# Products of the identity in TensorE's planned waits, and the rows of two more batches turned by VectorE and memory

## The chip, the cores and the metric

The kernel runs on one core of a Trainium2 chip. The metric is the time of one execution on the device, in microseconds (us); the median of several runs is quoted. The "granted clock" is the share of full speed that the profile shows for TensorE. "PSUM" is the program's name for the memory, in banks, that its TensorE products write to. Where two kernels are compared, "ratio" is the mean time of one kernel's runs over the mean of the other's runs of the same rounds on the same chip, so it is not quite the ratio of the medians; the 95% interval stands in brackets. "Start" and "last product" are times from the start of the profiled span.

## The reference

It is a stack of four graph-network layers on 32 batches of 512 nodes with 128 features, in float32. Every layer normalizes the rows, applies relu, calls a graph layer and adds the result to its input:

```python
for layer in (L0, L1, L2, L3):
    h = jnp.maximum(_layernorm(x), 0.0)
    x = x + layer(h, adj)
# L0: leaky_relu(norm(adj + I) @ (h @ W) + b)
# L1: elu(h @ W_in), elu(h @ W_out), elu(h @ W_node); adj @ in, adj.T @ out; tanh(concat @ W_upd)
# L2: four layers of row- and column-normalized adj with src, dst and self parts, with skips
# L3: m = tanh(adj @ (h @ W_msg)), then a GRU step of (m, h)
```

## The kernel before

The batches are independent. The program records every operation with its engine, an estimated duration and the buffers it uses; a list scheduler (`order`) then plans one order for all engines, in which the operations of several batches are mixed, and emits them in that order. In the trace of this kernel TensorE's 9594 records stand exactly in the planned order, also where the chip is slower than the plan (a wait of 1.29 us for `agg_in`, where the plan has no gap over 0.7 us) or faster (no wait ahead of the second and third fold, where it has one).

```python
class Plan:
    def op(self, engine, us, emit, reads=(), writes=(), kb=0.0, rank=None, later=0.0, land=0.0): ...
    def order(self):                       # an event loop: the engine that is idle takes the ready
        ...                                # operation of the lowest key that finds free buffers
        return done
```

Layers 1 to 3 need the normalized rows `h` also transposed, as `hT`. There are two ways to it. At the ends, where few batches are in flight, four TensorE transposes and a copy by ScalarE do it; in this kernel's trace the record of one transpose is 273 ns in the median, three in a row start 0.11 us apart, and the copy takes 0.59 us. In the middle VectorE turns 32x32 blocks (0.71 us for 128x512), four writes to memory (1.8 us each in the median, from issue to landing) and one read (2.7 us) put the blocks in their places, and ScalarE copies (0.62 us):

```python
        at_ends = b < 3 or b >= B - 2

        def transposed(h, name):
            if at_ends:
                ps, hT = plan.bank("t"), buf("s2", name=name)
                for c in range(NC):
                    op("PE", 0.109, lambda c=c: nc.tensor.transpose(ps.ap()[:, c * P:(c + 1) * P], h.ap()[:, c, :], ident),
                       [(h, {c}), ID], [(ps, {c})])
                op("ACT", t_act(N), lambda: nc.scalar.copy(hT.ap(), ps.ap()), [ps], [hT])
                return hT
            t, hT = turned(h, "turned"), buf("s2", name=name)
            op("ACT", t_act(N), lambda: nc.scalar.copy(hT.ap().rearrange("p (c a r) -> p c a r", c=NC, a=NC), turned_cols(t)), [t], [hT])
            return hT
```

One piece of layer 1 comes up later: ScalarE brings the sums `agg_in` and `agg_out` out of PSUM, for the products `upd`, and also copies the `rows` of norms, which only layer 2 needs.

```python
        op("ACT", t_act(N), lambda: nc.scalar.copy(agg_in.ap(), psi.ap()), [psi], [agg_in])
        ...
        op("ACT", t_act(2 * N), lambda: nc.scalar.copy(
            rows.ap().rearrange("p s (c n) -> p (s c) n", c=NC), spaced.ap().rearrange("p n k -> p k n")), [spaced], [rows])
```

## Time and profile before

| what | before |
|---|---|
| time, median of 3 runs | 2331.95 us (2329.25 to 2332.02) |
| profiled span | 2328.9 us |
| TensorE busy | 2293.4 us |
| TensorE's first real product | 11.06 us |
| end of TensorE's last product | 2321.50 us |
| mean granted clock | 0.997 |

TensorE is busy 98% of the span, so its own time line can be kept like an account. From the first real product to the end of the last one there are 2321.50 - 11.06 = 2310.4 us. Of these 2293.4 are busy, and the remaining 17.0 are waits. The tail after the last product is 7.4 us. The lines of the profile are in the prediction below, with how they are read; a line of the time line gives the start, the length, the engine and the line of the program, the operation, and in square brackets the idle time ahead of it and who ended it.

### The profile page before, as it was taken

The page shows a single profiled execution, that of the slowest core. Times are in us where ns is not written, and L with a number is a line of the kernel's source. Part 1 is how long each engine was busy: PE and PEld are TensorE (multiplying, and loading weights), DVE is VectorE, ACT ScalarE, POOL GpSimd, SP SyncE. Part 2 cuts the span into 40 slices and gives each one's busy share as a digit, 9 for nine tenths or more (in the row PEclk, how much of TensorE's full clock was granted, in tenths as well). Part 3 has the DMA queues.
Part 4 walks back from the last instruction along what each step waited for, and adds up shares of the span by engine and source line. Part 5 has one row for each costly group of instructions (what it writes and reads, how often), then busy time and mean ns, then how long its engine had stood idle before and what let it go on. Part 6 is the DMA issues. An engine that isn't in the chain of part 4 may idle for free.

```text
span 2328.9 us, 28035 instructions
## 1 busy us (share of the span) xinstructions
PE 2293.4 (98%) x9594; PEld 1438.1 (62%) x9594; DVE 1519.9 (65%) x4124; ACT 935.0 (40%) x2018; POOL 284.2 (12%) x218
## 2 busy tenths in 40 slices
PE   6999999999999999999999999999999999999998
PEld 4666666566665666666666666666656666666565
DVE  5556567666676776757766676666667667576754
ACT  7323434344343444434444333443434444344512
POOL 3001101111110111101111011111011111011101
PEclk9999999999999999999999999999999999999999
DMA  6202222323323133222233223232231332323100
GB/s 215 81 1 86 68 74 81 109 64 100 98 83 109 46 109 104 90 87 82 78 104 100 74 90 109 64 100 91 80 116 50 109 96 91 94 64 113 50 5 10
DMA packets 127295, 196.63 MB, mean 84 GB/s; under 512 B 18352, under 2 KB 75184, under 8 KB 127152
## 3 DMA queue, kind: packets, MB, share of 16 engines
q1 hardware_dynamic: 126864, 194.71, 27.2%
q8 instruction: 76, 1.25, 0.2%
q14 instruction: 67, 0.55, 0.1%
q10 hardware_dynamic: 288, 0.13, 0.0%
HBM read 157.95 MB, written 36.83 MB: 84 GB/s over the span
## 4 chain that ended last, share of the span: by engine, by line
PE 91%; DVE 3%; issue 2%; DMA 2%; ACT 1%; POOL 1%; SPq 0%; DVEq 0%; POOLq 0%; ACTq 0%
PE ps_agg L295 60%; PE ps_seven L566 12%; PE ps_sd L295 9%; PE ps_upd L295 3%; PE ps_gate L295 2%; PE ps_msg L295 1%; PE ps_lin L295 1%; PE ps_node L295 1%; DMA x<-in_x 0%; POOL inv L690 0%; ACT h L447 0%; DVE bn L419 0%; SPq L465 0%; DMA turned<-turn_turned 0%; DVE z L637 0%
## 5 line engine op out<-in xcount | busy, mean ns | idle before, releaser
L295 PE MATMUL ps_agg<-aT,sd 128*128 128x512 f32 x1024 | 509.6, 593 | 1.8 <-DVE sd L544 1.0
L295 PE MATMUL ps_agg<-a,sd 128*128 128x512 f32 x1024 | 489.4, 593 | 0.0
L435 POOL TENSOR_TENSOR sc<-v,neg_half 128x4 f32<-128x4 f32 (+1 forms) x128 | 170.0, 1328 | 1630.8 <-DVE v L422 1053.3
L295 PEld LDWEIGHTS ps_agg<-a,sd 128*128 128x128 f32 x1024 | 181.7, 190 | 158.3 <-issue 148.8
L447 ACT ACTIVATE h<-xr,nb,sc 128x128 f32<-128x128 f32 x384 | 158.2, 482 | 294.0 <-DVE nb L443 290.2
L295 PE MATMUL ps_agg<-f,w_sb 128*128 128x512 f32 x448 | 229.4, 594 | 0.0
L295 PEld LDWEIGHTS ps_agg<-aT,sd 128*128 128x128 f32 x1024 | 177.5, 191 | 75.1 <-issue 62.0
L295 PE MATMUL ps_sd<-w_sb,f 128*128 128x256 f32 x768 | 221.6, 381 | 1.8 <-ACT f L485 1.3
L566 PEld LDWEIGHTS ps_seven<-t_sb,s 128*128 128x128 f32 x1128 | 164.2, 191 | 67.9 <-issue 56.2
L295 PEld LDWEIGHTS ps_sd<-w_sb,f 128*128 128x128 f32 x768 | 137.5, 192 | 107.4 <-issue 85.0
L522 DVE TENSOR_TENSOR sd<-ps_sd,rf_sb 128x512 f32<-128x512 f32 x128 | 88.2, 689 | 145.2 <-PE ps_sd L295 144.5
L566 PE MATMUL ps_seven<-t_sb,s 128*128 128x128 f32 x1128 | 177.2, 275 | 0.0
L737 ACT ACTIVATE f<-ps_agg,cf_sb 128x512 f32<-128x512 f32 x128 | 87.4, 683 | 145.3 <-PE ps_agg L295 145.0
L295 PE MATMUL ps_agg<-aT,rep 128*128 128x512 f32 x256 | 130.9, 593 | 2.6 <-DVE rep L662 1.4
L295 PE MATMUL ps_agg<-a,rep 128*128 128x512 f32 x256 | 130.7, 592 | 0.0
L295 PE MATMUL ps_agg<-aT,msg 128*128 128x512 f32 x256 | 127.6, 593 | 0.0
L566 PEld LDWEIGHTS ps_seven<-w_sb,f 128*128 128x128 f32 x512 | 83.5, 191 | 55.7 <-issue 47.1
L690 POOL TENSOR_TENSOR inv<-stat,neg_half 128x8 f32<-128x8 f32 x32 | 64.7, 2022 | 370.5 <-DVE stat L689 370.5
L592 DVE TENSOR_TENSOR ev<-ps_seven,ev 128x512 f32<-128x512 f32 x94 | 64.6, 688 | 65.0 <-PE ps_seven L566 63.5
L607 ACT ACTIVATE sq<-a 128x512 f32<-128x512 f32 x128 | 79.9, 624 | 51.7 <-DMA a<-in_adj 50.3
L295 PE MATMUL ps_agg<-aT,h 128*128 128x256 f32 (+2 forms) x384 | 99.7, 380 | 0.0
L295 PEld LDWEIGHTS ps_agg<-f,w_sb 128*128 128x128 f32 x448 | 78.4, 191 | 27.8 <-issue 20.3
(142 smaller groups left out, 3781.9 us busy)
## 6 DMA issues: line engine op xcount, KB each, us to landing
aT<-in_adjt SPq DMA_DIRECT2D x124, 512.0 KB, 5.7
a<-in_adj SPq DMA_DIRECT2D x62, 512.0 KB, 5.5
turn_turned<-blk SPq DMA_DIRECT2D x324, 64.0 KB, 1.8
turned<-turn_turned SPq DMA_DIRECT2D x81, 256.0 KB, 2.7
spaced<-bounce SPq DMA_DIRECT2D x32, 512.0 KB, 4.8
x<-in_x SPq DMA_DIRECT2D x32, 256.0 KB, 2.8
out<-xo SPq DMA_DIRECT2D x30, 256.0 KB, 2.1
turn_f4r<-blk SPq DMA_DIRECT2D x108, 64.0 KB, 1.8
```

The costliest lines, as they stand in the source:

```text
L295: op("PE", t_mm(n), lambda: nc.tensor.matmul(out_of(ps.ap()), lhs(), rhs(), start=start, stop=stop), reads, [ps], later=later)
L435: op("POOL", t_pow(n), lambda: nc.gpsimd.tensor_tensor(inv.ap()[:, :n], v8.ap()[:, :n], neg_half[:, :n], op=ALU.pow), [v8, NH], [(inv, {0})])
L447: op("ACT", t_act(D, 2), lambda c=c: nc.scalar.activation(h.ap()[:, c, :], xin.ap()[:, c, :], AF.Relu, bias=nb.ap()[:, c:c + 1], scale=inv ...
L522: op("DVE", t_tt(N), lambda ps=ps, h=h: nc.vector.tensor_add(sd.ap()[:, 2 * h:2 * h + 2, :], ps.ap().rearrange("p (j v) -> p j v", j=2), s ...
L566: op("PE", t_mm(D), lambda j=j: nc.tensor.matmul(ps.ap()[:, k * H + j * D:k * H + (j + 1) * D], lhs()[:, j * P:(j + 1) * P], rhs(), start= ...
L592: op("DVE", t_tt(N), lambda: nc.vector.tensor_add(ev.ap(), bank_b.ap()[:, None, :H].to_broadcast([P, 2, H]), ev.ap()), [bank_b, ev], [ev])
L607: op("ACT", 0.73, lambda c=c: nc.scalar.activation(sq.ap(), a.ap()[:, c, :], AF.Copy, accum_out=stat.ap()[:, c:c + 1]), [(a, {c})], [sq, ( ...
L690: op("POOL", t_pow(2 * NC), lambda: nc.gpsimd.tensor_tensor(inv.ap(), stat.ap(), neg_half, op=ALU.pow), [stat, NH], [inv])
L737: op("ACT", t_act(N, 1), lambda ps=ps, i=i, f_new=f_new: nc.scalar.activation(f_new.ap(), ps.ap(), AF.Tanh, bias=cf_sb[:, i:i + 1]), [ps, ...
```

## The change

It has two parts. First, wherever the plan leaves TensorE idle for over 0.7 us, products of the identity with itself are emitted, as many as the plan says fit, into a PSUM bank that is free then; the result is never read. Their intent is to keep TensorE's clock up. `WARM` and `COLD` in the diff are the pace of one product: in before's trace the two records of a fold product take 0.22 us, from start to start, at full pace and 0.43 at half. `RISE` is the estimate of how long half pace lasts, where that trace has 5.5, 3.5 and about 6.8 us; `SHORT` is a choice. Second, batches 2 and 30 take the way through VectorE and memory, with 16 TensorE transposes fewer in each.

```diff
+    WARM, COLD, RISE, SHORT = 0.2225, 0.428, 3.5, 0.7
+    def kept_warm(self, done, product, begin):
+        banks = {x for o in done for x in o.bufs if x.kind == "bank"}
+        out, at, cold = [], begin, self.RISE
+        for o in done:
+            if o.engine == "PE":
+                gap = o.ready - at
+                if gap > self.SHORT:
+                    n = int(min(gap, cold) / self.COLD + max(gap - cold - 0.1, 0.0) / self.WARM)
+                    cold = 0.0
+                    used = {x.slot for x in banks if x.since < o.ready and x.until > at - 0.1}
+                    slot = next((k for k in range(self.places["bank"]) if k not in used), None)
+                    if slot is not None:
+                        out.append((slot, n))
+                at = o.ready + o.us
+            out.append(o)
 ... (emits out; the event loop notes o.ready, x.since and x.until)
-        at_ends = b < 3 or b >= B - 2
+        at_ends = b < 2 or b >= B - 1
 ...
+    def idle_products(slot, n):
+        ps = psum.tile([P, N], F32, name="ps_idle", tag=f"bank_{slot}", bufs=1)
+        for _ in range(n):
+            nc.tensor.matmul(ps[:, :P], ident, ident, start=True, stop=True)
 ...
-        for o in plan.order():
-            o.emit()
+        plan.kept_warm(plan.order(), idle_products, 1.3)
```

More of the change, by code (lines that the diff above doesn't have):

```diff
@@ L193, in order @@
                             free[buf.kind].append(buf.slot)
+                            buf.until = now
                     unfinished[o.batch] -= 1
@@ L209, in order @@
                     for x in new:
-                        x.slot = free[x.kind].pop(0)
+                        x.slot, x.since, x.until = free[x.kind].pop(0), now, None
                 for item in held:
@@ L215, in order @@
                 done.append(o)
+                o.ready = now
                 idle_at[e] = now + o.us
@@ L225, in order @@
         return done
+    WARM, COLD, RISE, SHORT = 0.2225, 0.428, 3.5, 0.7
[14 more added lines that the diff above has]
+            out.append(o)
+        for o in out:
+            if isinstance(o, tuple):
+                product(*o)
+            else:
+                o.emit()
 @with_exitstack
```

## The prediction

> **What bounds the kernel now.** I read four views in this order: busy times, TensorE's waits, the windows with the granted clock, and TensorE's timeline at the two ends. The first is the page's line of busy time.
>
> ```profile
> PE 2293.4 (98%) x9594; PEld 1438.1 (62%) x9594; DVE 1519.9 (65%) x4124; ACT 935.0 (40%) x2018; POOL 284.2 (12%) x218
> ```
>
> TensorE (PE) is busy 98% of a span of 2328.9 us, so its 35.5 us without work are nearly all that waiting can give back. The view of waits, cut to TensorE and the first 60 us, shows where most of them lie:
>
> ```profile
> PE ps_fold L295 <- DMA raw<-in_raw: 11.1, 1, 11.1
> PE ps_t L483 <- ACT h L447: 4.5, 2, 3.1
> PE ps_lin L295 <- ACT agg L632: 1.4, 2, 0.7
> PE ps_upd L295 <- ACT agg_in L667: 1.3, 1, 1.3
> PE ps_agg L295 <- DVE v L609: 1.1, 1, 1.1
> PE ps_sd L295 <- ACT hT L485: 0.8, 1, 0.8
> PE ps_sd L295 <- ACT f L485: 0.7, 1, 0.7
> ```
>
> 11.1 us are the first load, some 9.8 are waits in batches 0 to 2. From 60 to 2170 us the same view lists only 2.8 us; from 2170 on it has 4.1 us (1.4 on `rep`, the rest under 0.8 each), and after TensorE's last product, at 2321.5, comes a tail of 7.4 us that the change does not touch. In the middle nothing is to be had but TensorE's own work.
>
> Busy is not full speed. Windows (stretch, length, busy time and count of PE, PEld, DVE, ACT, POOL, then the clock):
>
> ```profile
> 30.00:33.50 3.50, 3.50 (x8) 2.75 (x9) 0.97 (x3) 2.55 (x8) 0.00 (x0) 0.52 0.87 250
> 55.40:61.00 5.60, 4.90 (x10) 2.90 (x11) 4.29 (x27) 5.34 (x14) 2.61 (x3) 0.52 0.64 154
> 61.00:90.00 29.00, 29.00 (x88) 15.56 (x87) 15.95 (x39) 15.60 (x31) 3.30 (x2) 1.00 0.39 141
> ```
>
> In two stretches the granted clock is 0.52. A third is not in that column (1.00 there), but the timeline shows it. Each float32 product has two records, so x12 is six products:
>
> ```profile
> 11.06 2.93 PE L295 MATMUL ps_fold<-raw 128*128 128x128 f32 x12 [11.06 <-DMA raw<-in_raw]
> ...
> 21.72 1.50 PE L295 MATMUL ps_fold<-raw 128*128 128x128 f32 x12
> ...
> 30.00 3.68 PE L295 MATMUL ps_sd<-w_sb,hT 128*128 128x256 f32 x8 [0.75 <-ACT hT L485]
> ...
> 76.16 1.03 PE L295 MATMUL ps_sd<-w_sb,hT 128*128 128x256 f32 x4
> ```
>
> Six products of one form take 2.93 us at 11 us and 1.50 at 22, that is about 0.43 and 0.22 us each from start to start. The half pace lasts from 11.06 to about 16.6.
>
> [...] half pace for 5.5, 3.5 and about 6.8 us. [...] it was at half clock at 30.0 us after gaps of 1.41 and 0.75 us, not one long gap. [...] VectorE's turn (0.711 us for 128x512) needs four writes to memory of 1.8 us and a read of 2.7 us after it, from issue to landing. [...] records here are 273 ns, but three in a row start 0.11 us apart, and that is the cost to the stream.
>
> **The change, part by part.** The built program's order shows 79 products of the identity: 33 ahead of the first real product, then groups of 3, 4, 5, 4, 5, 6 and 10 in batches 0 to 2, and 5 and 4 near the end. 32 transposes leave TensorE (80 before, 48 after), 8 turns are added on VectorE (108 to 116). Nothing else is added to TensorE.
>
> (1) Clock. First stretch: 5.5 us at half pace become 2.75, provided inputs are there: the last part of `h` is done at 14.26 and of `diag` at 14.24, and the chunk that needs them would start at about 16, so yes. Gain 2.75. Second: the four `sd` products take 3.50 us from start to start; warm, at 0.43 each, 1.72. Gain 1.8. Third: from 57.73 to 61.07, 3.34 us hold products that need 1.72 warm; the transposes before them run at ScalarE's pace and gain nothing. Gain 1.6. Sum 6.15 us. The chain of batch 0 runs from TensorE through ScalarE and VectorE back to TensorE here, so I count all of it.
>
> (2) What the products of the identity cost where they are too many. The identity is ready at 1.34 us. If the clock rises after 3.5 us, 33 products take 8 x 0.428 + 25 x 0.2225 = 9.0 us and end at 10.6, before the load at 11.02; if after 6.8 us, 16 x 0.428 + 17 x 0.2225 = 10.6, ending at 12.2. I take a loss of 0.35. The groups of 4 and 5 ahead of the second and third fold are 2.0 us, where the trace shows no wait at the folds and 1.41 just after: loss 0.6. 4 ahead of `sd` are 0.9 against a wait of 0.75, 6 ahead of `lin` 1.3 against 0.68, before a long gap anyway: together 0.35. Loss 1.3; (1) and (2) leave 4.85.
>
> (3) Transposes: 32 x 0.11 = 3.5 us off an engine that is never idle in between. The turns add 8 x 0.711 = 5.7 us to VectorE (65% busy), and their wait of some 6 us lies behind other batches' products, as for batches 3 to 29 now.
>
> (4) Waits. I built the products of the identity alone, without the turns, to read its order: 90 products, among them 14 where now are 10, a group of 4 after that which is gone, and 5, 4 and 3 near the end where now are 5 and 4. The first real product after the 10 is now batch 2's own aggregation, moved up because its path has become longer. So 11 products, 11 x 0.2225 = 2.4 us, is what the new order expects to wait less. The trace's waits at those places (3.07 and 0.67 near 55 us, 3.9 from 2180 to 2200) make it plausible. I take 2.2.
>
> Sum: 4.85 + 3.5 + 2.2 = 10.6 us, 0.45%. 2331.95 - 10.6 = 2321.4; I say 2321.
>
> **The rivals.**
> (a) A wait takes the place of the one removed: in the first 60 us the end is set by loads and by ScalarE, not TensorE. For: ScalarE is busy 9.68 of 10 us from 40 to 50 and 9.18 from 50 to 60, memory moves over 400 GB/s from 11 to 20. Against: ScalarE waits 0.95, 0.44 and 1.76 us between 30 and 40 for results that come earlier now, and the loads of batch 1 are in by 24. It would cut (1) to half: 2324 to 2325.
> (b) The products of the identity get in the way: they stand in program order, and a real product that is ready earlier has to wait. For: the groups ahead of the folds. Against: 46 of them after the start are 10.2 us in all and replace waits of 9.8 + 4.1. All in the way by a third: 2324.
> (c) The turns of batches 2 and 30 add waits of 5 to 6 us where too few batches are in flight. For: batch 30 has only batch 31 beside it at the end. Against: batch 31 is at work then, and the order has just one planned gap there. If two turns show: 2331.
> (d) The clock stays low in spite of them, so that (1) is lost and only 4 us remain: 2328. Against: they are ordinary products.
>
> **Range and chances.** The three times before span 2.8 us. Each rival takes 3 to 10 us and none is likely to hold in full; the other way, waits at both ends could shrink by 4 more. So 2315 to 2327. Two per cent is 46.6 us, more than all of TensorE's idle time: same is nearly certain.
>
> **What would show it.** Right: no clock under 0.9 between 11 and 90 us; the four first `sd` products in 1.9 us; the first fold at 11 to 12 us; batch 0's aggregation done near 17.5 instead of 20; 48 transposes; TensorE's waits of the first 60 us mostly filled; the waits from 2170 on cut from 4.1 us to about 2. Wrong: the first fold later than 12.2; `ps_sd` or `ps_msg` waiting for `turned` in batch 2 or 30 for over 2 us; a mean clock under 0.99 from 20 to 60 us; TensorE's last product less than 6 us earlier than 2321.5.

## The result

The changed kernel took 2319.45 us (2317.86 to 2320.76, 6 runs) against 2330.71 us of the kernel before in the same rounds. The ratio is 0.9951 [0.9938, 0.9964]: 0.5% faster, within the 2% that count as the same. In the profile the span went from 2328.9 to 2316.1 us, the mean clock from 0.997 to 0.999. The page's line of busy times, after:

```profile
PE 2301.4 (99%) x9720; PEld 1450.3 (63%) x9720; DVE 1521.2 (66%) x4132; ACT 933.6 (40%) x2018; POOL 284.1 (12%) x218
```

TensorE is busy 8.0 us longer although the span is 12.8 us shorter, because the products of the identity count as busy. The view of waits of the first 60 us had seven lines before, the first of them the 11.1 us of load. What is left of it now, whole:

```profile
PE ps_idle L862 <- POOL ident masks.py:199: 1.4, 1, 1.4
PE ps_upd L324 <- ACT agg_in L696: 1.2, 1, 1.2
PE ps_agg L324 <- ACT h L476: 0.8, 1, 0.8
```

TensorE's time line, at the three stretches that ran at half clock before, shows the 33 first products (66 records), the folds, and the `sd` products:

```profile
1.40 9.96 PE L862 MATMUL ps_idle<-ident 128*128 128x128 f32 x66 [1.40 <-POOL ident masks.py:199]
11.41 1.61 PE L324 MATMUL ps_fold<-raw 128*128 128x128 f32 x12
...
28.22 1.99 PE L324 MATMUL ps_sd<-w_sb,hT 128*128 128x256 f32 x8
```

Six fold products take 1.61 us instead of 2.93, and the `sd` products 1.99 instead of 3.68. The windows (clock third from the end) agree, with 1.00 where there was 0.52:

```profile
30.00:33.50 3.50, 3.44 (x17) 2.17 (x16) 3.50 (x16) 3.42 (x9) 1.19 (x1) 1.00 0.97 323
55.40:61.00 5.60, 5.60 (x24) 3.65 (x23) 3.18 (x11) 5.35 (x16) 0.19 (x2) 1.00 0.74 254
```

Near the end, where batch 30 starts, TensorE's time line before was:

```profile
2180.53 1.16 PE L295 MATMUL ps_lin<-w_sb,agg 128*128 128x128 f32 x8 [0.68 <-ACT agg L632]
2182.34 1.48 PE L483 MATMUL ps_t<-ident,h 128*128 128x128 f32 x4 [0.65 <-ACT h L447]
2184.50 1.13 PE L295 MATMUL ps_sd<-w_sb,f 128*128 128x256 f32 x4 [0.68 <-ACT f L485]
...
2197.30 1.10 PE L295 MATMUL ps_agg<-aT,rep 128*128 128x512 f32 x2 [1.45 <-DVE rep L662]
...
2299.54 1.40 PE L483 MATMUL ps_t<-ident,h 128*128 128x128 f32 x4
```

and after:

```profile
2179.17 1.28 PE L862 MATMUL ps_idle<-ident 128*128 128x128 f32 x10
2180.29 1.03 PE L324 MATMUL ps_sd<-w_sb,f 128*128 128x256 f32 x4
...
2187.23 1.05 PE L324 MATMUL ps_lin<-w_sb,agg 128*128 128x128 f32 x8
...
2294.38 0.60 PE L512 MATMUL ps_t<-ident,h 128*128 128x128 f32 x4
```

The four waits in brackets are gone, and so are both groups of transposes that took 1.48 and 1.40 us. Four transposes without a wait take 0.60 us, as the last line shows. Before, they took so long because ScalarE delivered `h` in four pieces: at 2182.34 the four records of 0.328 us start 0.38 us apart, beside ScalarE's 1.65 us for the pieces. This is waiting that the profile counts as busy.

**The account of TensorE.** "Products" are those of the identity after the first group, at 0.2225 us each; "work" is the busy time without any of them; "waits" is the rest up to the last product. The account is made from one profile of each kernel and adds up to the last product.

| kernel | first real product | work | waits | products | last product |
|---|---|---|---|---|---|
| before | 11.06 | 2293.4 | 17.0 | 0 | 2321.5 |
| after | 11.41 | 2281.2 | 5.8 | 10.2 | 2308.7 |

So the gain of 12.8 us in the profile is nearly all in the work (-12.2). Waits and products together are 16.0 us where the waits alone were 17.0.

### The profile page after: what moved, and what is told of

It is laid out like the page before. It is cut to its first block, busy times and chain, and to the rows that moved or that the text cites.

```text
span 2316.1 us, 28365 instructions
## 1 busy us (share of the span) xinstructions
PE 2301.4 (99%) x9720; PEld 1450.3 (63%) x9720; DVE 1521.2 (66%) x4132; ACT 933.6 (40%) x2018; POOL 284.1 (12%) x218
## 4 chain that ended last, share of the span: by engine, by line
PE 92%; DVE 3%; DMA 2%; ACT 1%; SPq 1%; issue 1%; POOL 0%; DVEq 0%; ACTq 0%; POOLq 0%
PE ps_agg L324 60%; PE ps_seven L595 12%; PE ps_sd L324 9%; PE ps_upd L324 3%; PE ps_gate L324 2%; PE ps_msg L324 1%; PE ps_lin L324 1%; PE ps_node L324 1%; DMA turned<-turn_turned 1%; SPq L494 1%; PE ps_idle L862 1%; DMA turn_turned<-blk 0%; DVE bn L448 0%; DMA x<-in_x 0%; DMA spaced<-bounce 0%
```

## The experiments

Twelve runs were made, in three groups of four, each with five rounds; all gave correct results. The groups ran on three different chips, on which the kernel before had means of 2332.3, 2332.1 and 2333.7 us. How far one kernel's profiles differ shows in the change itself, profiled twice: last product at 2308.65 and 2309.42 us. So differences of about 1 us between two profiles say nothing. A profile is also only one of a kernel's runs, and these spread by 1.1 to 6.2 us, so that even a few microseconds between two profiles can be chance. The accounts below are read with that in mind.

### The two parts apart: e1 to e4

e1 has the products alone, with the plan and the ways of before:

```diff
-        at_ends = b < 2 or b >= B - 1
+        at_ends = b < 3 or b >= B - 2
```

> The products of the identity (90 of them) without the turns of batches 2 and 30. Theory A (the prediction's sum: clock 4.85 net of overruns, transposes 3.5, waits 2.2): 4.9 us faster than before, 2326. Rival B (the clock is hidden behind loads and ScalarE, the gain of the whole change is the turns'): at most 2.4 us faster, 2328. Both expect the near-end waits of before (lin, t, sd and rep of batch 30) to be still there, the first three filled with products. A expects no granted clock under 0.9 from 28 to 62 us and the first aggregation done near 17.7 us.

Measured: 2328.39 us, ratio 0.9985 [0.9972, 0.9997]. By the means, 3.6 us less than before: between A's 4.9 and B's 2.4. A had excluded a clock under 0.9 from 28 to 62 us; there was one, from 42.2 us on (below).

e2 has the turns alone:

```diff
-        plan.kept_warm(plan.order(), idle_products, 1.3)
+        for o in plan.order():
+            o.emit()
```

> The turns of batches 2 and 30 without any product of the identity. Theory A: 5.7 us faster than before (2325), half pace at 11 to 16.6, near 30 and near 54 us as before. Rival B: 9 us or more faster (2321 or less). Theory C (new, from the trace of after: transposes that wait for ScalarE's chunks cost 1.4 to 1.6 us for four and not 0.44, so batch 30's transposes cost more than predicted): 7.5 to 8 us faster, and no wait of TensorE over 0.5 us from 2175 to 2195 but one.

Measured: 2324.0 us, ratio 0.9962 [0.995, 0.9975], 8.8 us less than before by the means: far over A's 5.7, and between C's 8 and B's 9.

e3 and e4 are the whole change with only batch 2 and with only batch 30 turned:

```diff
-        at_ends = b < 2 or b >= B - 1
+        at_ends = b < 2 or b >= B - 2     # e3
+        at_ends = b < 3 or b >= B - 1     # e4
```

> The change with batch 2 turned but batch 30 not. Theory A (waits and transposes shared evenly by the two batches, 2.85 us each): 3 us slower than the whole change, 2322.5. Theory C (batch 30's transposes stand alone at ScalarE's pace, two times about 1.0 us lost, and its waits of 3.9 us): 5 us slower than the whole change, 2324.5, and from 2175 to 2200 the waits of before.

> The change with batch 30 turned but batch 2 not. Theory A: 3 us slower than the whole change, 2322.5. Theory C: 2 to 3 us slower (1.75 us of transposes and under 1 us of waits near 50 us, since the 3.5 us of batch 2's aggregation that fill the wait there would have been done anyway), 2322.

Measured: e3 2327.22 us, ratio 0.9977 [0.9964, 0.9989]; e4 2322.82 us, ratio 0.9958 [0.9945, 0.9972]. Against e1, turning batch 2 is worth 1.8 us and turning batch 30 is worth 5.9 us, by the means on the same chip. The first is not clear of noise (the runs are 2324.4 to 2328.9 us in e3, 2327.9 to 2330.4 in e1); the second is. The even split of theory A is refuted: e3 came out 5 us over its 2322.5 and 3 over C's 2324.5. e4 fits both, which were too close to tell apart. e3's profile is of its slowest run.

The account shows what each part does:

| kernel | first real product | work | waits | products | last product |
|---|---|---|---|---|---|
| e1, products alone | 10.99 | 2287.2 | 8.7 | 12.7 | 2319.6 |
| e2, turns alone | 10.60 | 2288.0 | 15.1 | 0 | 2313.7 |
| e3, batch 2 | 11.98 | 2285.8 | 11.2 | 10.9 | 2319.8 |
| e4, batch 30 | 11.06 | 2283.6 | 8.0 | 12.0 | 2314.6 |

In e1 the work is 6.2 us less than before, and most of that is the clock's doing; 0.6 us is the group of transposes near 2181 us, which took 1.48 and takes 0.92 with the clock at 1.00 in both. But the waits fall by only 8.3 us, while 12.7 us of products come in: 4.4 us of the 6.2 are lost again (0.9 of it by the wait for `agg_in`, which was 2.23 instead of 1.29 us by chance, see below). So these products gave back nothing of the waits they stand in; on the account they took 4.4 us more. Around batch 30 e1 shows how:

```profile
2178.08 1.28 PE L862 MATMUL ps_idle<-ident 128*128 128x128 f32 x10
2179.19 1.06 PE L324 MATMUL ps_lin<-w_sb,agg 128*128 128x128 f32 x8
2180.09 1.06 PE L862 MATMUL ps_idle<-ident 128*128 128x128 f32 x8
2181.29 0.92 PE L512 MATMUL ps_t<-ident,h 128*128 128x128 f32 x4
...
2195.37 1.10 PE L324 MATMUL ps_agg<-aT,rep 128*128 128x512 f32 x2 [1.59 <-DVE rep L691]
```

In place of the first two waits of before, of 0.68 and 0.65 us, stand groups of five and four products (1.1 and 0.9 us), each longer than its wait, and the wait for `rep`, ahead of which the plan has no products, stays at 1.59. In the changed kernel other work of batches 30 and 31 stands in all these places.

From e1 to after, which adds both turns, the work falls by 6.0 us and waits with products by 5.4 us. The 32 transposes at 0.11 us are 3.5 us of the first. Some 1.1 us are the hidden wait for ScalarE's pieces in batch 30's groups (0.92 and 1.40 us in e1, against 0.60 each in a stream). And 1.6 us come from a fall of the clock in e1's profile.

What the turn of batch 2 moves is visible at the wait for `h`, which was 3.07 us ahead of four transposes of 1.63 us. Before:

```profile
55.43 1.63 PE L483 MATMUL ps_t<-ident,h 128*128 128x128 f32 x4 [3.07 <-ACT h L447]
57.73 2.07 PE L295 MATMUL ps_sd<-w_sb,f 128*128 128x256 f32 x4 [0.67 <-ACT f L485]
```

After:

```profile
49.14 2.40 PE L862 MATMUL ps_idle<-ident 128*128 128x128 f32 x20
52.33 0.46 PE L324 MATMUL ps_agg<-diag,h 128*128 128x128 f32 x2 [0.79 <-ACT h L476]
...
53.71 0.33 PE L512 MATMUL ps_t<-ident,h 128*128 128x128 f32 x1
53.88 0.60 PE L324 MATMUL ps_agg<-aT,h 128*128 128x256 f32 x2
```

Batch 2's aggregation now lies between the transposes, so TensorE works while ScalarE makes the next piece. e1 stands for the same place without a turn: 14 products, the four transposes, 4 products, then `sd`.

That fall of the clock, which theory A had excluded, comes right after the wait for `agg_in`, which no product fills because the plan does not see it (time line, then the window with the clock 0.55):

```profile
42.28 0.80 PE L324 MATMUL ps_upd<-w_sb,agg_in 128*128 128x128 f32 x2 [2.23 <-ACT agg_in L696]
```

```profile
42.30:46.00 3.70, 3.70 (x19) 3.70 (x20) 3.70 (x7) 3.70 (x12) 0.00 (x0) 0.55 0.00 0
```

From here to `lin` of batch 1 e1 needs 8.32 us and the changed kernel 6.74 for the same products, which is the 1.6 us. e3 had the same wait, 2.23 us too, with the clock at 1.00 after it. So the same wait did and did not cost the clock. Its length has two values, with a sign that goes with them: 2.23 to 2.29 us in the profiles of e1, e3, e10 and e11, in which GpSimd's power operation for batch 1's `h` (128x8 elements, near 32 to 36 us) took 3.29 us, and 1.1 to 1.3 us in before, after, e2, e4 to e7 and e9, in which it took 1.94. Why it takes longer in some runs is not shown. Nor does the fall decide e1's time: its runs with a mean clock of 0.998, the profiled one among them, took 2328.4 and 2328.8 us, those with 0.999 took 2327.9 to 2330.4.

### The products in halves: e5 and e6

e5 keeps the turns and only the 33 first products; e6 keeps the turns and only the 46 of the later groups:

```diff
-                    if slot is not None:
+                    if slot is not None and at == begin:                        # e5
+                    if slot is not None and any(o.engine == "PE" for o in out): # e6
```

> The whole change, but of the products of the identity only the 33 ahead of the first real product. Theory A (each part of the clock is worth what its cold stretch took): the cold stretches near 28 to 34 and 54 to 58 us come back; they cost 1.8 us and at most 1 us, less 1 us of overruns saved: 1.5 to 2 us slower than the whole change, 0.9957. Rival D (after a warm start the waits of batches 0 to 2 are too short to lower the clock): no clock under 0.9 anywhere and as fast as the whole change or 1 us faster, 0.995.

> The whole change without the 33 products at the start, the other 46 kept. Theory A: half pace from the first fold for 3 to 6 us, the first aggregation done 1.3 to 2.4 us later than 17.7, no cold stretch after that; 1 to 2 us slower than the whole change, 0.9957. Rival D (the loads and ScalarE hide the start): the first aggregation is later but batch 0's rep aggregation starts at 32.2 us as in the whole change, and the time is the same.

Measured: e5 2318.02 us, ratio 0.9941 [0.9928, 0.9953]; e6 2317.21 us, ratio 0.9937 [0.9925, 0.9949]. Each half, with the turns, does at least as well as both (0.9951), and the last products agree within 0.11 us: 2308.76 in e5, 2308.65 in e6, 2308.65 after. Each theory had half of it right. A's clock came true (e5 is at half clock from 27.6 to 34.4 and from 54.9 to 58.3 us, e6 nowhere after its start), but not its loss of 1 to 2 us; D's time came true, but neither its full clock in e5 nor its start of batch 0's `rep` aggregation in e6 (33.42 us, not 32.2).

| kernel | first real product | work | waits | products | last product |
|---|---|---|---|---|---|
| e5, first 33 only | 11.79 | 2286.0 | 11.0 | 0 | 2308.8 |
| e6, later 46 only | 10.52 | 2281.9 | 6.0 | 10.2 | 2308.7 |

What the later groups win in clock (2286.0 to 2281.2 of work, from e5 to after) they cost in time (11.0 of waits become 16.0 of waits and products). e5 has the half clock again at the `sd` products:

```profile
28.17 3.78 PE L324 MATMUL ps_sd<-w_sb,hT 128*128 128x256 f32 x8 [0.75 <-ACT hT L514]
```

What it costs at the start is not there at the end. Batch 0's eight last aggregation products of layer 2 start at 62.75 us after and at 65.91 in e5, 3.2 us later; at the end 0.1 us of this is left. Between 62 and 2165 us the changed kernel waits 3.2 us and e5 1.2 us, and near the end the changed kernel has 2.0 us of products and 0.2 us of waits where e5 has 1.1 us of waits. (3.2 - 1.2) + (2.2 - 1.1) = 3.1. That is where the difference goes, and not yet why: waits of the middle do not follow the start in the other profiles (e2, nearly as late as e5 with 65.09 us, waits 4.5 us there, and e7, early with 61.94, waits 1.6). It may be chance.

### Fewer and more products: e7 and e8

e7 starts with 30 products instead of 33, has none ahead of the second and third fold, where before's trace shows no wait, and 3 instead of 6 ahead of batch 1's `lin`:

```diff
+                    seen = sum(isinstance(y, tuple) for y in out)
+                    n = {0: 30, 2: 0, 3: 0, 6: 3}.get(seen, n)
```

> The whole change with 30 products at the start instead of 33, none ahead of the second and third fold (4 and 5 before), 3 instead of 6 ahead of batch 1's lin. If products ahead of a real product that is ready are lost time (the prediction's point 2): the first h of batch 0 starts 0.4 to 0.5 us earlier on ScalarE, batch 0's rep aggregation at 31.7 instead of 32.25, batch 1's lin 0.4 us earlier still; 0.5 to 1 us faster than the whole change, 0.9948. If the clock falls in the wait that is left between the folds and the transposes (near 25 us), 1 us slower, 0.9957, and a clock of 0.5 near 26 to 30 us.

Measured: 2314.46 us, ratio 0.9928 [0.9915, 0.9942], the lowest so far; last product 2305.06. On its chip it is 2.2 us faster than e6 and 3.1 us faster than e5, by the means. Its account is first product 10.81, work 2280.4, waits 6.3 and products 7.6: against after 0.6 us at the start, 0.8 of work and 2.1 of waits and products. The 0.6 can be chance: its first fold waits 0.66 us for the load, and without any first products that load let the first fold start at 10.45 to 11.06 us. The gain was more than the 0.5 to 1 us expected (0.9948), `rep` started at 31.45 us, and the clock did not fall, although the wait of 1.42 us ahead of the transposes came back.

e8 doubles every group but the first:

```diff
-                        out.append((slot, n))
+                        out.append((slot, 2 * n if any(isinstance(y, tuple) for y in out) else n))
```

> The whole change with every group of products but the first doubled (92 instead of 46). If nearly all of TensorE's time in batches 0 to 2 is on the path (theory A), 46 x 0.2225 = 10.2 us less the wait of 0.8 left after the group of 10: 8 to 9.5 us slower than the whole change, 0.999. Rival D (ScalarE and loads set the pace there, TensorE has slack): under 5 us slower, 0.997 or less. It gives the price of one product that stands in the way.

Measured: 2322.78 us, ratio 0.996 [0.9947, 0.9972]. TensorE then waits for nothing in the first 62 us but the identity:

```profile
PE ps_idle L862 <- POOL ident masks.py:199: 1.4, 1, 1.4
```

Its account is first product 10.55, work 2279.1, waits 2.7 and products 20.5. So of the 10.2 us of added products 3.1 took the place of waits and 7.1 came on top; an earlier first product (0.9) and less work (2.1) took 3.0 of these back, and the last product ends at 2312.84, 4.2 us later than after. Too many products do cost, but less than their length. That is under the 5 us of rival D and half of what theory A had (8 to 9.5).

### On one chip, and a better one: e9 to e12

After and the turns alone once more, so that the worth of the products is taken on one chip:

> The changed kernel once more, so that it stands on one chip with the next three. If nothing but noise parts the runs: 0.9945 to 0.9957 of before, as at first (0.9951), and TensorE's last product at 2308.3 to 2309 us. Theory: the products of the identity give, with the turns in, about 5 us in the profile and 3 to 5 us in time over the next kernel; the rival, that most of what they give at the start is given back later and only the turns count, has under 2.5 us.

> The turns alone, no products of the identity. Theory: 0.9960 to 0.9972 of before, 3 to 5 us over the changed kernel. Rival (the products are worth under 2.5 us where the turns are in): 0.9951 to 0.9961. A half clock again in parts of 10 to 60 us in both.

e9 is the changed kernel unedited and e10 has e2's edit. Measured: e9 2320.63 us, ratio 0.9946 [0.9933, 0.996]; e10 2322.91 us, ratio 0.9957 [0.9945, 0.997]. By the means the products are worth 3.0 us where the turns are in, and the turns alone 10.2 us. That is the lower edge of what the theory expected for the products, and e10's ratio missed its range and lies in the rival's; with intervals this wide, 3.0 against the rival's under 2.5 is not settled, and the runs of the two overlap (2318.6 to 2322.3 and 2320.0 to 2326.1). In the profiles it is 3.9 us (last product at 2309.42, just over the range, and 2313.34). All are under the 4.85 predicted. e10 has half clock at 30 to 33, 47 to 50 and 57 to 60 us; e9 has none.

e11 is e7 without the groups of 5 and 4 near the end:

```diff
-                    n = {0: 30, 2: 0, 3: 0, 6: 3}.get(seen, n)
+                    n = {0: 30, 2: 0, 3: 0, 6: 3, 8: 0, 9: 0}.get(seen, n)
```

> The trimmed kernel of before (30 products at first, none ahead of the second and third fold, 3 ahead of batch 1's lin) with the last two groups, 5 and 4 near the end, left out as well. They take 1.05 and 0.9 us; where they were absent, the trace showed waits of 1.1 us in their place. Theory that they are more than the waits they fill: 0.8 to 1.0 us less than the trimmed kernel, so 0.9922 to 0.9927 of before, last product at about 2304.2. Rival, that they cost nothing because the wait comes anyway: 0.9928, last product at 2305.0.

Measured: 2316.98 us, ratio 0.9928 [0.9916, 0.994], equal to e7's, as the rival had it. The two last groups cost nothing that can be measured: the waits come back in their place (1.0, 0.8 and 0.3 us). e11's profiled run was the slowest of its five (2313.38 to 2319.58). In it `upd` waited 2.23 us for `agg_in`, which ScalarE copied after the 2.0 us of `rows` (time lines of TensorE, then of ScalarE):

```profile
41.72 0.49 PE L326 MATMUL ps_upd<-w_sb,agg_in 128*128 128x128 f32 x2 [2.23 <-ACT agg_in L698]
```

```profile
39.18 2.01 ACT L735 COPY rows<-spaced 128x1024 f32<-128x1024 f32 x1
41.09 0.57 ACT L698 COPY agg_in<-ps_agg 128x512 f32<-128x512 f32 x1
```

The clock is 0.56 from 42.3 to 46.0 us in this run. In e7 ScalarE has the same order, yet the wait was 1.24 us and the clock stayed at 1.00. What differs is GpSimd's operation ahead of `h`, which ScalarE makes before `rows` (e7, then e11):

```profile
31.51 1.94 POOL L466 TENSOR_TENSOR sc<-v,neg_half 128x8 f32<-128x8 f32 x1 [7.09 <-DVE v L640]
31.55 3.29 POOL L466 TENSOR_TENSOR sc<-v,neg_half 128x8 f32<-128x8 f32 x1 [7.11 <-DVE v L640]
```

That is 1 us of wait and some 1.6 us of pace in a profile whose last product came 4.5 us later than e7's. But e11's other run with a mean clock of 0.998 took 2315.85 us, so it is not shown that this makes the slow runs slow.

e12 is e11 with batch 0's copy of `rows` kept behind `agg_in` and `agg_out`. A `10: 0` is added to e11's table (not shown), so that there are again no groups near the end:

```diff
-            ... spaced.ap().rearrange("p n k -> p k n")), [spaced], [rows])
+            ... spaced.ap().rearrange("p n k -> p k n")), [spaced] + [agg_out] * (b == 0), [rows])
```

> As the kernel just before this one, and batch 0's copy of the normed rows (ScalarE, 2.0 us) kept behind the copies of agg_in and agg_out, which TensorE waits for at upd (1.2 us in the trace, unfilled). Theory: that wait goes, upd starts 1.0 to 1.3 us earlier (about 39.6), and about half of it is left at the end: last product 0.4 to 0.8 us earlier than in that kernel, 0.9918 to 0.9925 of before. Rival, that the rows come 2 us later and hold up batch 0's layer of f, since the plan is also a different one after it: no gain, 0.9923 to 0.9930.

Measured: 2317.45 us, ratio 0.9931 [0.9918, 0.9943]. The order is the wanted one:

```profile
40.51 0.49 PE L326 MATMUL ps_upd<-w_sb,agg_in 128*128 128x128 f32 x2 [0.93 <-ACT agg_in L698]
```

```profile
39.90 0.57 ACT L698 COPY agg_in<-ps_agg 128x512 f32<-128x512 f32 x1
40.36 0.58 ACT L702 COPY agg_out<-ps_agg 128x512 f32<-128x512 f32 x1
...
41.46 2.05 ACT L735 COPY rows<-spaced 128x1024 f32<-128x1024 f32 x1
```

The wait is 0.93 us, although GpSimd's operation took 3.29 us here too, which went with 2.23 us or more in every profile with `rows` in front (`agg_in` is copied at 39.90 us, in e11 at 41.09). No half clock follows. So the new order does shorten this wait, but the mean time is no better than e11's: the theory's gain at the end was missed, and the rival (no gain, 0.9923 to 0.9930) is the nearer. The plan as a whole came out differently: batch 2's aggregation no longer stands in the wait for batch 0's `h`, and there are waits of 1.07 us ahead of batch 1's `lin`, 0.32 ahead of the transposes and 0.76 ahead of `sd`. What e12 has is less spread: 1.1 us over five runs, where e11 has 6.2 and e9 3.7. Five runs are few for that, and it is not shown that the order of `rows` is its cause.

The kernels with trimmed products (e7, e11) are the fastest. On one chip e11's mean is 3.8 us below that of the changed kernel (2316.7 against 2320.5).

## Why the prediction was right, and where its terms were not

The predicted 2321.0 us and range held: 2319.45 us, a gain of 11.3 us by the medians where 10.6 were worked out (13.2 by the means of e9's rounds). Its signs came true: the clock was 1.00 in all windows from 11 to 90 us, the first fold started at 11.41, the aggregation of batch 0 was done at 17.7, the four `sd` products took 1.83 us from start to start, the waits from 2170 us on fell to 0.2 (beside 2.0 us of products), and TensorE's last product came 12.8 us earlier. The waits of the first 60 us were filled but for 2.0 us after the identity. The sum held because terms were wrong in opposite directions, and that is luck.

- **Term (1), the clock: right.** 6.15 us were predicted from three stretches. From the first fold to batch 0's aggregation TensorE took 5.14 us before and 2.67 in e1; the `sd` products, from start to start, 3.50 and 1.83; the third stretch 3.34 and 1.79. That is 5.7 us. e1's work fell by 6.2 us, in spite of a new fall of the clock that cost 1.6, so some 2 us came from elsewhere. At least half of that is in transposes, which were to gain nothing: the four at 55.43 took 1.63 us before and 1.06 in e1, those at 2182.34 1.48 and 0.92.
- **Term (2), products that are too many: too small.** 1.3 us were predicted from comparing groups with waits at single places. In e1, with 57 products after the start, waits and products are 4.4 us more than the waits alone were, 3.5 without the chance at `agg_in`. The products by themselves gave 3.6 us (e1) and 3.0 us on top of the turns (e9 against e10), where (1) and (2) had 4.85.
- **Term (3), the transposes: too small.** 3.5 us were counted from 0.11 us each. From e1 to after the work fell by 6.0 us. Of these 1.6 are e1's fall of the clock, so 4.4 are the turns', 0.9 more than predicted. The prediction took the distance in a stream, but two of batch 30's groups follow ScalarE's pieces, as the 1.48 and 1.40 us of before show against 0.60. That wait was invisible in the list of waits.
- **Term (4), waits that the turns fill: too small.** 2.2 us were predicted from 11 products fewer in the plan. From e1 to after, waits with products fell by 5.4 us: those 11 are 2.4 of it, and 2.9 are waits, of which the chance of the wait for `agg_in` (2.23 and 1.2 us) is 1.0. Without the products the turns took only 1.9 us of waits (before to e2). Taken together, an estimate without the two pieces of chance in e1's profile (1.6 us of clock and 0.9 to 1.0 of wait) is that the last product came 4.4 us earlier from before to e1, where (1) and (2) had 4.85, and 8.3 us earlier from e1 to after, where (3) and (4) had 5.7. By the means of the runs it is the same picture: the turns were worth more than predicted, the products somewhat less. The turns alone measured 8.8 (e2) and 10.2 (e10). The accounts do not explain all of that: e2's work fell by 5.4 us, and its half pace at the start lasted 2.7 us where before's lasted 5.5, in the profiles at hand.

Rival (b), products in the way, was the one that held most: it guessed a third of the later products in the way, 3.4 us, and e1 lost 4.4. It loses 0.9 of that if the chance at `agg_in` is left out. Rival (a) is not settled. e1, which has before's order, is 2.6 us ahead of before at batch 0's eight products (63.04 against 65.59 us) and 1.9 at the last one, so most of it stays; between e5 and after 3.2 us shrink to 0.1. Rival (c), waits of 5 to 6 us, did not come, but it is not nothing: TensorE waits for the copy of a turned `hT` for 0.3 us in all from 62 to 400 us, for 0.76 at 2121.7, where the planned order points to batch 30's first one, and for 0.2 from 2165 us on. The wait near 2122 us was 1.20 in e9, 1.53 in e2 and 1.77 in e10, and absent in e5, e6 and e8. Rival (d) is refuted by the clock.

What was missed altogether is the wait for `agg_in`. The prediction listed its 1.3 us and did not ask who stood in front of it: a copy by ScalarE that another layer needs, and before that an operation of GpSimd whose length varies between runs (1.94 or 3.29 us).

Two observations at the start stay without a cause. The half clock at the `sd` products follows, in before and in e5, a stretch of little but transposes, with two waits of 1.41 and 0.75 us in it in both; the eight records take 3.68 and 3.78 us, and 1.99 in the changed kernel, where both waits are gone. The change uses ordinary products, which had gone with a rise in before: its first six fold products took 2.93 us, the next six 1.50. No run has transposes alone without waits, so what they do to the clock is not shown. And before and after agree on a VectorE operation on 128x4 elements (`sc`, for batch 1) that takes 0.15 us in the median: here it took 1.22 us before (from 38.09 us) and 1.23 after (from 34.63), ending within 0.03 us of the GpSimd operation beside it, which took 1.61 us in both. Why is not shown. It lies on the way to batch 1's `h`, so it bears on the waits of the start.

## What to carry to other kernels

Filler that keeps a clock up should be judged by the account of work, waits and filler. It saved no waiting here (in e1 8.3 us of waits made way for 12.7 us of products), and it cost time where there was too much of it (in e8 10.2 us more of products ended 4.2 us later), so try fewer than the plan says (e7 and e11, with ratios of 0.9928, were faster than the full number with 0.9951 and 0.9946). Real work in a wait gave time back: where another way of doing something lets another batch's products into a gap, as the turn of batch 30 did (5.9 us, by the means of e1 and e4), look for that first. And groups of short dependent instructions that are much longer than their stream time, as the four transposes of 1.48 us against 0.60, hid waits that the list of waits did not show.

## What the traces show of the clock and of busy time

- The length of a gap alone does not tell whether the clock falls to half. A gap of 2.23 us was followed by a fall in e1 (0.55 from 42.3 to 46.0 us) and in e11 (0.56), and was not in e3 (1.00).
- The moment of the rise varied by some 3 us. The products of the identity start at 1.40 us in every profile that has the first group; their records from 1.40 to 4.40, to 7.40 and to 10.40 us number 14, 16 and 28 in e3, which is full pace only after about 6 us, 14, 21 and 29 in the changed kernel's profile, full pace after about 5, and in e9 already 14 and 29 in the first two, full pace after about 3 us. The whole group of 33 takes 9.05 us in e9, 9.96 in the changed kernel's profile and 10.33 in e5.
- A group of transposes at the pace of another engine's pieces shows as busy: four took 1.48 us with a start every 0.38 us, against 0.60 us in a stream.
